# Differential attention with a feed-forward part on one core: the values product by Strassen's seven products

## The chip, the core and the metric

The kernel runs on one core of one Trainium2 chip. The metric is the device time of one execution in microseconds. Every engine of the core (TensorE for matmuls, VectorE, ScalarE, GpSimd) works through its own list of instructions in order, and SyncE issues most DMAs in the order of its own queue. In the profile they are PE, DVE, ACT, POOL and SP.

## The reference

The input x has 2048 tokens of 256 numbers, in float32. What is computed, cut to what matters:

```python
def attn(h):                       # h = layernorm(x)
    qkv = h @ Wqkv_w.T + Wqkv_b
    # 16 query heads as 8 pairs, 8 key heads as 4 pairs, D = 128; values 4 x 256
    p1 = softmax(causal(q[..., 0] @ k[..., 0].T / sqrt(D)))
    p2 = softmax(causal(q[..., 1] @ k[..., 1].T / sqrt(D)))
    o = (p1 - lam * p2) @ v        # 8 query pairs; two of them share keys and values
    o = o * rsqrt(mean(o * o) + eps) * subln_w * (1 - lambda_init)
    return o.reshape(S, 2048) @ out_w.T + out_b
x = x + layernorm(attn(layernorm(x)))
x = x + layernorm(ffn(layernorm(x)))   # Hadamard transforms, silu(gate) * up, down; 256 -> 1024 -> 256
```

## The kernel before

The work goes in four groups (`g`), one for each pair of key heads with its values. For a group, queries, keys and values of all 2048 tokens are projected from the normalised input (`project_heads`, `project_values`); two query pairs share the group's keys, and the program interleaves the rows of both, so that a tile of 128 tokens gives two half tiles of 64 tokens by two pairs.

The attention runs unit by unit. A `Unit` is one tile of 128 tokens for the first eight tiles (both halves, `ns` = 2), and one half tile for the other eight, so a group has 24 units and the whole kernel 96. The first group goes from short rows to long, the others from long to short. In the step of a unit, these things stand in each engine's list:

- `scores` (L267): matmuls of the unit's queries with all keys up to the diagonal, for two softmaxes, into PSUM tiles `sc` of 1024 columns, of which there are three. VectorE empties each into `e` and keeps the running minimum (L282, L293); ScalarE takes the exponential (L308).
- `combine` (L340): VectorE forms e0 + cf * e1 for the unit before.
- `turn` and `arrive` (L360, L365, L375): the probabilities are turned around for the values product, in blocks of 32x32 on VectorE and by a write to DRAM (`dr`) and four reads back (`pt`).
- `values` (L391), for the unit three steps back (`LAG`): for every tile of 128 keys a matmul with the turned probabilities as weights and the values as the moving operand, 128 rows by 256 columns, added up in a PSUM tile `po`.
- ScalarE copies the result and sums its squares (L404, L407), GpSimd forms the factor and scales (`inverse`, L418 to L421), `turn_out` and `arrive_out` turn the result around by VectorE and DRAM (L434, L439, L449), `project_out` multiplies it with the output weights (L458), and `accumulate` adds it to `acc` (L468).

The order is written out by hand: the tables `before`, `mid`, `between` and `after` say at which step a projection, a part of the folding of the feed-forward weights (`transform`, L618, on GpSimd, in steps 7 to 35), or a piece of the feed-forward part stands. The feed-forward part runs on blocks of 256 tokens, from the last block to the first, and begins while the last units are worked on.

Of the kernel before, what the change touches and what calls it, by code (L numbers as in the profile page):

```python
# [16 lines left out]
P = 128  # L17
# [15 lines left out]
LAG = 3  # L33
# [15 lines left out]
def kernel(  # L49
# [58 lines left out]

    x2 = x.rearrange("(b t s q) d -> b s q t d", t=2, s=2, q=64)
    outv = out.rearrange("(b t s q) d -> b s q t d", t=2, s=2, q=64)  # L110


    with ExitStack() as actx:
# [6 lines left out]
        ps_s = actx.enter_context(tc.tile_pool(name="ps_s", bufs=3, space=PSUM))  # L120
        ps_o = actx.enter_context(tc.tile_pool(name="ps_o", bufs=2, space=PSUM))
# [3 lines left out]
        qT = [qkp.tile([P, NT, 2, 2, 64], F32, name=f"q{m}") for m in range(2)]  # L125
        kT = [qkp.tile([P, S], F32, name=f"k{m}") for m in range(2)]
        vt = qkp.tile([P, NT, HID], F32, name="v")

# [4 lines left out]
        loaded = {}  # L133

        def load_qkv(g, engines, count=4):

            if g not in loaded:
                wq = xtp.tile([P, 2, 1024], F32, tag="wq", name=f"wq_{g}")
                loaded[g] = wq, xtp.tile([P, 256], F32, tag="vb", name=f"vb_{g}"), list(range(4))
            wq, _, left = loaded[g]  # L140
            for _ in range(count):
                k = left.pop(0)
                engines[k % len(engines)].dma_start(wq[:, :, ts(k, 256)], wqkv[4 * g + k])

        def load_vbias(g):
            nc.gpsimd.dma_start(loaded[g][1], vbias[:, ts(g, 256)].to_broadcast([P, 256]))
# [10 lines left out]

        def scale_wo(g):
            for c in range(2):
                nc.vector.tensor_scalar(  # L160
                    wos[g][:, :, c, :],
                    wos[g][:, :, c, :],
                    colv[:, C_SUBLN + c : C_SUBLN + c + 1],
                    1.0 - LAMBDA_INIT,
                    ALU.mult,
                    ALU.mult,
                )

        def project_heads(g, nb, j2, both=True, n=512):

            wq = loaded[g][0]
            cols4 = ts(nb, n)
            xb, lo = divmod(nb * n, 512)
            nt = n // P
            pp = ps_s.tile([P, 1024], F32, tag="sc", name=f"pp_{g}_{nb}_{j2}_{n}")
            for h in range(2):
                j = 2 * j2 + h
                for c in range(2):
                    nc.tensor.matmul(  # L179
                        pp[:, 512 * h : 512 * h + n],  # L180
                        lhsT=wq[:, c, ts(j, P)],
                        rhs=xnT[:, xb, c, lo : lo + n],
                        start=(c == 0),
                        stop=(c == 1),
                    )
            for h in range(2):
# [4 lines left out]
                if j < 4:  # L191
                    dst = qT[h][:, ts(nb, nt), :, j2, :].rearrange("d t s q -> d (t s) q")
                    src = src.rearrange("d (t q) -> d t q", q=64)
                else:
                    dst = kT[h][:, cols4]
# [6 lines left out]
        def project_values(g, nb):  # L202

            wq, vb, _ = loaded[g]
            pp = ps_s.tile([P, 1024], F32, tag="sc", name=f"pv_{g}_{nb}")
            for t in range(4):
                for c in range(2):
                    nc.tensor.matmul(  # L208
                        pp[:, ts(t, 256)],
                        lhsT=xnT[:, nb, c, ts(t, P)],  # L210
                        rhs=wq[:, c, 768:1024],
# [6 lines left out]
                vb.unsqueeze(1).to_broadcast([P, 4, 256]),  # L218
                ALU.add,
            )  # L220


        class Unit:
            def __init__(self, g, i, subs):
                self.g, self.i, self.subs = g, i, subs
                self.ns = len(subs)
                self.nk = i + 1
                self.L = [i * P + 64 * (s + 1) for s in subs]
                self.at = [a * self.nk * P for a in range(self.ns)]

                self.ng = self.nk if self.ns == 2 else (self.nk + 1) // 2
                self.n = f"{g}_{i}_{subs[0]}"
# [19 lines left out]
        def scores(u, half):  # L252

            for a, m in u.half(half):
# [5 lines left out]
                for c, w in enumerate(cuts(L)):  # L260
# [4 lines left out]
                    for k, lo in enumerate(los):  # L265
                        ww = w - lo if k == len(los) - 1 else step
                        nc.tensor.matmul(  # L267
                            sc[:, 512 * k : 512 * k + ww],
                            lhsT=qT[m][:, u.i, u.subs[a]].rearrange("d p q -> d (p q)"),
# [35 lines left out]
        def exponentials(u, half):  # L305
# [10 lines left out]
            if half:  # L316

                u.ed = sm.tile([P, 2], F32, tag="ed", name=f"ed_{u.n}", bufs=8)
                nc.scalar.activation(
                    u.ed[:, : u.ns], u.d[:, : u.ns, 0], AF.Square, scale=16.0 * math.sqrt(EPS)  # L320
                )

        def pad(u):

            lo, hi = u.L[0], (u.at[1] if u.ns == 2 else 256 * u.ng)
            if hi > lo:
                nc.gpsimd.memset(u.es[0][:, lo:hi], 0.0)
# [16 lines left out]
        def move(u, moved):  # L344

            if u:
                turn(u)
            if moved:
                arrive_out(moved)
            if u:  # L350
                arrive(u)

        def turn(u):
# [3 lines left out]
            e, x = u.es  # L357
            ng = u.ng
            order = "p (r g c) -> p r g c" if u.ns == 2 else "p (g r c) -> p r g c"
            nc.vector.transpose(  # L360
                x[:, : 256 * ng].rearrange("p (g c r) -> p r g c", g=ng, r=2),
                e[:, : 256 * ng].rearrange(order, g=ng, r=2),
            )
            dr = dram.tile([NT // 2, 4, 32, 4, 64], F32, tag="dr", name=f"dr_{u.n}")
            nc.sync.dma_start(  # L365
                dr[:ng].rearrange("g b q a w -> (b q) g (a w)"),
                x[:, : 256 * ng].rearrange("p (g w) -> p g w", g=ng),
            )
            u.dr = dr

        def arrive(u):
            ng, dr = u.ng, u.dr
            u.pt = ep.tile([P, S], F32, tag="pt", name=f"pt_{u.n}")
            for a in range(4):
                nc.sync.dma_start(  # L375
                    u.pt[ts(a, 32), : 256 * ng].rearrange("p (k w) -> p k w", w=64),
                    dr[:ng, :, :, a, :].rearrange("g b q w -> q (g b) w"),
                )

        def values(u, part=None):  # L380

            whole = [(a, kc) for a in range(u.ns) for kc in range(u.nk)]
            cut = len(whole) // 2
            if part != 1:
                u.po = None
            todo = whole if part is None else (whole[:cut], whole[cut:])[part]
            u.po = u.po or ps_o.tile([P, 512], F32, tag="o", name=f"po_{u.n}")
            ptv = u.pt[:, : 256 * u.ng].rearrange("p (g q r) -> p g r q", q=P, r=2)
            for a, kc in todo:
                g, r = (kc, a) if u.ns == 2 else (kc // 2, kc % 2)  # L390
                nc.tensor.matmul(  # L391
                    u.po[:, ts(a, HID)],
                    lhsT=ptv[:, g, r, :],
                    rhs=vt[:, kc, :],
                    start=(kc == 0),
                    stop=(kc == u.i),
                )
            if part == 0:
                return

            if (u.g, u.i) not in outs:
                outs[u.g, u.i] = op.tile([P, 2, HID], F32, tag="osb", name=f"osb_{u.g}_{u.i}")
            u.osb = outs[u.g, u.i][:, u.subs[0] : u.subs[0] + u.ns, :]
            nc.scalar.copy(u.osb.rearrange("p s e -> p (s e)"), u.po[:, : u.ns * HID])  # L404
            u.ss = sm.tile([P, 2], F32, tag="ss", name=f"ss_{u.n}")
            for a in range(u.ns):
                nc.scalar.activation(  # L407
                    u.po[:, ts(a, HID)],
                    u.po[:, ts(a, HID)],
                    AF.Square,  # L410
                    accum_out=u.ss[:, a : a + 1],
                )

        def inverse(u):

            f = sm.tile([P, 2], F32, tag="f", name=f"f_{u.n}")
            w = sm.tile([P, 2], F32, tag="u", name=f"u_{u.n}")
            nc.gpsimd.tensor_tensor(w[:, : u.ns], u.ss[:, : u.ns], u.ed[:, : u.ns], ALU.add)  # L418
            nc.gpsimd.tensor_tensor(f[:, : u.ns], w[:, : u.ns], mhalf[:, : u.ns], ALU.pow)  # L419
            for a in range(u.ns):  # L420
                nc.gpsimd.tensor_scalar(  # L421
                    u.osb[:, a, :], u.osb[:, a, :], f[:, a : a + 1], 16.0, ALU.mult, ALU.mult
                )

        outs = {}

        def complete(u):
            return u and u.subs[-1] == 1

        def turn_out(u):  # L430

            osb = outs[u.g, u.i]
            xo = op.tile([P, 512], F32, tag="xo", name=f"xo_{u.n}", bufs=1)
            nc.vector.transpose(  # L434
                xo.rearrange("p (g c r) -> p r g c", g=2, r=2),
                osb.rearrange("p r (g c) -> p r g c", g=2),
            )
            dr = dram.tile([2, 4, 32, 4, 64], F32, tag="do", name=f"do_{u.n}")
            nc.sync.dma_start(  # L439
                dr.rearrange("g b q a w -> (b q) g (a w)"),  # L440
                xo.rearrange("p (g w) -> p g w", g=2),
            )
            u.do = dr

        def arrive_out(u):
            dr = u.do
            u.oT = op.tile([P, 2, 2, P], F32, tag="oT", name=f"oT_{u.n}")
            for a in range(4):
# [592 lines left out]
```

## Time and profile before

| | |
|---|---|
| median of three runs | 1440.66 us (1440.43 to 1441.46) |
| span of the profiled execution | 1438.7 us |
| its own time beside the span | not listed on the page |
| busy: PE, DVE, ACT, POOL | 1429.8, 1028.8, 507.9, 360.9 us |
| largest groups on PE | values L391 488.1 us, scores L267 478.2, projections L179 170.6, output projection L458 121.0 |
| DMA | 210.79 MB, mean 147 GB/s |

A line of a group names the source line, the engine, the operation, what it writes and reads, the shapes and the count, then busy time and the mean duration in nanoseconds, then the idle time before it and what ended it. A line of the waits names who waited for whom, the total, the number of times and the longest. The profiled execution is one more run of the same program; its span goes from the first to the last instruction.

### The profile page before, as it was taken

The page shows a single profiled execution, that of the slowest core. Times are in us where ns is not written, and L with a number is a line of the kernel's source. Part 1 is how long each engine was busy: PE and PEld are TensorE (multiplying, and loading weights), DVE is VectorE, ACT ScalarE, POOL GpSimd, SP SyncE. Part 2 cuts the span into 40 slices and gives each one's busy share as a digit, 9 for nine tenths or more (in the row PEclk, how much of TensorE's full clock was granted, in tenths as well). Part 3 has the DMA queues.
Part 4 walks back from the last instruction along what each step waited for, and adds up shares of the span by engine and source line. Part 5 has one row for each costly group of instructions (what it writes and reads, how often), then busy time and mean ns, then how long its engine had stood idle before and what let it go on. Part 6 is the DMA issues. An engine that isn't in the chain of part 4 may idle for free.

```text
span 1438.7 us, 17597 instructions
## 1 busy us (share of the span) xinstructions
PE 1429.8 (99%) x5436; PEld 1037.6 (72%) x5436; DVE 1028.8 (72%) x2285; ACT 507.9 (35%) x1114; POOL 360.9 (25%) x683
## 2 busy tenths in 40 slices
PE   9999999999999999999999999999999999999998
PEld 7567767756766777776677776675777777888887
DVE  6588798847656888644967779545877799766774
ACT  3453433323133334333433334323424445531111
POOL 2037724830028921011111111111111121121110
PEclk9999999999999999999999999999999999999999
DMA  5379889856667797832788887631999999732120
GB/s 147 73 169 202 195 179 219 178 93 139 149 135 146 162 214 173 169 86 63 155 183 180 170 201 165 132 81 52 210 202 193 193 191 190 170 94 81 52 59 15
DMA packets 501436, 210.79 MB, mean 147 GB/s; under 512 B 396032, under 2 KB 499456, under 8 KB 501216
## 3 DMA queue, kind: packets, MB, share of 16 engines
q1 hardware_dynamic: 498128, 200.73, 65.9%
q0 software_dynamic: 2352, 8.26, 2.1%
q8 instruction: 44, 0.72, 0.2%
q10 hardware_dynamic: 864, 0.68, 0.2%
q14 instruction: 48, 0.39, 0.1%
HBM read 111.05 MB, written 98.57 MB: 146 GB/s over the span
## 4 chain that ended last, share of the span: by engine, by line
PE 98%; DVE 1%; DMA 0%; POOL 0%; issue 0%; ACT 0%; POOLq 0%; DVEq 0%
PE po L391 32%; PE sc L267 31%; PE pp L179 11%; PE pout L458 8%; PE gu L721 8%; PE pd L756 4%; PE pv L208 4%; DMA vb<-in_vbias 0%; PE warm L494 0%; DVE e L282 0%; DVE e L340 0%; DVE e L360 0%; DVE v L215 0%; PE pst L523 0%; ACT q L198 0%
## 5 line engine op out<-in xcount | busy, mean ns | idle before, releaser
L391 PE MATMUL po<-v,pt 128*128 128x256 f32 x2176 | 488.1, 379 | 0.0
L267 PE MATMUL sc<-k,q 128*128 128x512 f32 (+7 forms) x1280 | 478.2, 519 | 1.5 <-DVE last L293 0.6
L391 PEld LDWEIGHTS po<-v,pt 128*128 128x128 f32 x2176 | 425.7, 196 | 59.6 <-issue 11.1
L267 PEld LDWEIGHTS sc<-k,q 128*128 128x128 f32 x1280 | 237.8, 190 | 214.3 <-issue 182.4
L308 ACT ACTIVATE e<-e,last 128x192 f32<-128x192 f32 (+28 forms) x256 | 299.5, 1171 | 221.6 <-DVE last L293 202.6
L282 DVE TENSOR_SCALAR_CACHE_REDUCE e<-sc 128x1024 f32<-128x1024 f32 (+15 forms) x248 | 231.2, 932 | 176.6 <-PE sc L267 175.7
L418 POOL TENSOR_TENSOR u<-ss,ed 128x1 f32<-128x1 f32 (+1 forms) x96 | 20.0, 208 | 747.1 <-ACT po L407 747.0
L404 ACT COPY osb<-po 128x256 f32<-128x256 f32 (+1 forms) x96 | 42.6, 444 | 465.2 <-PE po L391 464.2
L340 DVE SCALAR_TENSOR_TENSOR e<-e,cf,e 128x64 f32<-128x64 f32 (+31 forms) x128 | 173.9, 1380 | 3.4
L360 DVE STREAM_TRANSPOSE e<-e 128x1536 f32<-128x1536 f32 (+7 forms) x96 | 166.7, 1737 | 7.4 <-DVE e L340 0.5
L179 PE MATMUL pp<-xnT,wq 128*128 128x512 f32 (+1 forms) x408 | 170.6, 568 | 0.3 <-DVE xnT L510 0.3
L179 PEld LDWEIGHTS pp<-xnT,wq 128*128 128x128 f32 x408 | 77.0, 190 | 78.3 <-issue 74.8
L458 PE MATMUL pout<-wo,oT 128*128 128x256 f32 x512 | 121.0, 379 | 0.1
L282 DVE TENSOR_SCALAR_CACHE_REDUCE e<-sc,mx 128x320 f32<-128x320 f32 (+13 forms) x128 | 97.1, 759 | 21.0 <-PE sc L267 8.0
L458 PEld LDWEIGHTS pout<-wo,oT 128*128 128x128 f32 x512 | 97.2, 190 | 13.2 <-issue 0.4
L293 DVE CUSTOM_DVE_ANT_0 e<-sc,mask,mx 128x64 f32<-128x64 f32 x248 | 70.5, 284 | 8.8
L734 ACT ACTIVATE hT<-gu,colv 128x256 f32<-128x256 f32 x64 | 26.9, 471 | 120.5 <-PE gu L721 120.5
L721 PE MATMUL gu<-fxnT,wgate 128*128 128x256 f32 x256 | 65.7, 379 | 0.0
L721 PE MATMUL gu<-fxnT,wup 128*128 128x256 f32 x256 | 65.7, 379 | 0.0
L421 POOL TENSOR_SCALAR osb<-osb,f 128x256 f32<-128x256 f32 x128 | 62.7, 490 | 11.8
L419 POOL TENSOR_TENSOR f<-u,mhalf 128x1 f32<-128x1 f32 (+1 forms) x96 | 58.3, 608 | 7.5
L740 DVE SCALAR_TENSOR_TENSOR hT<-gu,colv,hT 128x256 f32<-128x256 f32 x64 | 30.6, 478 | 40.5 <-ACT hT L734 40.5
(101 smaller groups left out, 1097.5 us busy)
## 6 DMA issues: line engine op xcount, KB each, us to landing
dr<-e SPq DMA_DIRECT2D x20, 1024.0 KB, 4.7
pt<-dr SPq DMA_DIRECT2D x80, 256.0 KB, 5.8
dr<-e SPq DMA_DIRECT2D x20, 896.0 KB, 4.4
pt<-dr SPq DMA_DIRECT2D x80, 224.0 KB, 5.0
do<-xo SPq DMA_DIRECT2D x64, 256.0 KB, 4.1
oT<-do SPq DMA_DIRECT2D x256, 64.0 KB, 2.6
dr<-e SPq DMA_DIRECT2D x20, 768.0 KB, 4.4
pt<-dr SPq DMA_DIRECT2D x80, 192.0 KB, 4.3
```

Of the source, the lines that this page charges most:

```text
L179: nc.tensor.matmul(pp[:, 512 * h : 512 * h + n], lhsT=wq[:, c, ts(j, P)], rhs=xnT[:, xb, c, lo : lo + n], start=(c == 0), stop=(c == 1),)
L267: nc.tensor.matmul(sc[:, 512 * k : 512 * k + ww], lhsT=qT[m][:, u.i, u.subs[a]].rearrange("d p q -> d (p q)"), rhs=kT[m][:, at + lo : at + ...
L282: nc.vector.tensor_scalar(dst, src, 1.0, best, ALU.mult, ALU.min, accum_out=u.mx[:, k0, c : c + 1],)
L293: nc.vector.tensor_tensor_reduce(e[:, L - 64 : L], sc[:, tail : tail + 64], mask, 1.0, best, ALU.add, ALU.min, accum_out=u.last[:, k0 : k0 ...
L308: nc.scalar.activation(e, e, AF.Exp, bias=u.last[:, 2 * a + m : 2 * a + m + 1], scale=-1.0, accum_out=u.d[:, a, m : m + 1],)
L340: nc.vector.scalar_tensor_tensor(e0, e1, cf[:, a : a + 1], e0, ALU.mult, ALU.add)
L360: nc.vector.transpose(x[:, : 256 * ng].rearrange("p (g c r) -> p r g c", g=ng, r=2), e[:, : 256 * ng].rearrange(order, g=ng, r=2),)
L391: nc.tensor.matmul(u.po[:, ts(a, HID)], lhsT=ptv[:, g, r, :], rhs=vt[:, kc, :], start=(kc == 0), stop=(kc == u.i),)
L419: nc.gpsimd.tensor_tensor(f[:, : u.ns], w[:, : u.ns], mhalf[:, : u.ns], ALU.pow)
L421: nc.gpsimd.tensor_scalar(u.osb[:, a, :], u.osb[:, a, :], f[:, a : a + 1], 16.0, ALU.mult, ALU.mult)
L458: nc.tensor.matmul(u.pout[:, :HID], lhsT=u.oT[:, c, p, :], rhs=wos[u.g][:, p, c, :], start=(p == 0 and c == 0), stop=(p == 1 and c == 1),)
L721: nc.tensor.matmul(ps[:, ts(2 * j + n, 256)], lhsT=ffn[which][:, c, ts(fc, P)], rhs=xnT[:, c, :], start=(c == 0), stop=(c == 1),)
```

## The change

The unit of the values product becomes a block of 256 tokens (two tiles, with their two query pairs as rows `r`) against a block of 256 keys. A block on the diagonal takes six matmuls of 256 columns. A block off the diagonal (there are 28 in a group) is taken as a product of two 2x2 matrices of 128-wide blocks, by seven products in the form of Strassen and Winograd. Values are now the weights and the probabilities the moving operand, so the result arises transposed.

- The sums of the values, `vm`, are formed by GpSimd after each `project_values`; the sums of the probabilities, `sums`, by GpSimd for each block, four additions of 256 columns, up to two blocks ahead (`NSUM`).
- Turned probabilities are fetched block by block (`fetch`), up to five blocks ahead (`NA`), after all units of a block of rows have been turned.
- The products gather in four PSUM banks, `z0` to `z3`. For them, `sc` has two tiles instead of three. `collect` puts the result together on ScalarE, VectorE and GpSimd once for each block of rows (32 in all).
- The output need not be turned any more. The sum of its squares runs along partitions now, and is formed by squares on ScalarE, a transpose and a reduction on VectorE, and a way through DRAM in small transfers (`squares`, `scales`); the factor is applied after the output projection.
- Queries are kept in a ring of two blocks of 512 tokens, and are projected shortly before they are used.
- These later steps are put into the program by a clock that counts the matmuls' time (`later`, `poll`). Projections, folding steps and the begin of the feed-forward part move by some steps, and its back product uses the `z` banks.

The core of the diff:

```diff
-LAG = 3
+NA = 5
+NSUM = 2
+RIPE = 3
-        ps_s = actx.enter_context(tc.tile_pool(name="ps_s", bufs=3, space=PSUM))
-        ps_o = actx.enter_context(tc.tile_pool(name="ps_o", bufs=2, space=PSUM))
+        ps_s = actx.enter_context(tc.tile_pool(name="ps_s", bufs=2, space=PSUM))
+        ps_z = actx.enter_context(tc.tile_pool(name="ps_z", bufs=1, space=PSUM))
...
+            nc.gpsimd.tensor_tensor(t1, b12, b11, ALU.subtract)
+            nc.gpsimd.tensor_tensor(t2, b22, t1, ALU.subtract)
+            nc.gpsimd.tensor_tensor(t4, b21, t2, ALU.subtract)
+            nc.gpsimd.tensor_tensor(t3, b22, b12, ALU.subtract)
...
+        def sums(n):
...
+            nc.gpsimd.tensor_tensor(s1, a21, a22, ALU.add)
+            nc.gpsimd.tensor_tensor(s2, s1, a11, ALU.subtract)
+            nc.gpsimd.tensor_tensor(s4, a12, s2, ALU.subtract)
+            nc.gpsimd.tensor_tensor(s3, a11, a21, ALU.subtract)
...
+        def values(n):
+            b, j = items[n]
+            p = b.p[j]
+            if j < b.i:
+                s, v, m = b.s[j], vv[:, j], vm[:, j]
+                last = j == b.i - 1
+                product(b, 0, 0, v[:, 0, 0, :], p[:, 0, 0], last)
+                product(b, 2, 0, v[:, 1, 0, :], p[:, 0, 1], False)
+                product(b, 2, 256, m[:, 3, :], p[:, 1, 1], False)
+                product(b, 1, 0, m[:, 0, :], s[:, 0, :], last)
+                product(b, 0, 256, m[:, 1, :], s[:, 1, :], last)
+                product(b, 3, 0, vv[:, j, 1, 1, :], s[:, 3, :], False)
+                product(b, 1, 256, m[:, 2, :], s[:, 2, :], last)
+                return
...
+        def collect(b):
...
+                nc.scalar.copy(w[:, 0, :], b.z[0][:, :256])
+                nc.scalar.copy(w[:, 1, :], b.z[1][:, :256])
+                nc.vector.tensor_tensor(w[:, 2, :], b.z[0][:, 256:], w[:, 0, :], ALU.add)
+                nc.vector.tensor_tensor(w[:, 3, :], b.z[1][:, 256:], w[:, 2, :], ALU.add)
+                nc.gpsimd.tensor_tensor(
+                    b.o[:, 1],
+                    w[:, 2:4, :],
+                    w[:, 1:2, :].to_broadcast([P, 2, 256]),
+                    ALU.add,
+                )
+                nc.vector.tensor_tensor(
+                    b.o[:, 0], b.z[2].rearrange("p (r q) -> p r q", r=2), w[:, 0::3, :], ALU.add
+                )
+                nc.vector.tensor_tensor(o1, b.z[3], o1, ALU.add)
...
+            b.sq = op.tile([P, 1024], F32, tag="sq", name=f"sq_{b.n}", bufs=1)
+            nc.scalar.activation(b.sq, b.o.rearrange("p h r q -> p (h r q)"), AF.Square)
+            nc.gpsimd.tensor_tensor(b.sq[:, :512], b.sq[:, :512], b.sq[:, 512:], ALU.add)
+            later(3.0, squares, b)
...
         for which, begin_at, steps in (
-            ("up", 5, range(7, 15)),
-            ("gate", 17, (18, 19, 20, 21, 22, 22, 23, 23)),
+            ("up", 7, range(8, 16)),
+            ("gate", 18, (19, 20, 20, 21, 22, 22, 23, 23)),
             ("down", 26, (28, 29, 29, 30, 30, 31, 32, 33, 34, 35)),
         ):
```

## The prediction

> **What bounds the kernel now.** I read the page's engine totals and its chain first. In the busy line, each engine has its busy time, its share of the span and its instructions; the second line is the chain that ended last, by engine.
>
> ```profile
> span 1438.7 us, 17597 instructions
> PE 1429.8 (99%) x5436; PEld 1037.6 (72%) x5436; DVE 1028.8 (72%) x2285; ACT 507.9 (35%) x1114; POOL 360.9 (25%) x683
> ...
> PE 98%; DVE 1%; DMA 0%; POOL 0%; issue 0%; ACT 0%; POOLq 0%; DVEq 0%
> ```
>
> TensorE is the bound from end to end. A busy TensorE need not be at its peak, so next comes the chain in order of time (start, length, what):
>
> ```profile
> 340.00 3.43 PE sc L267 x8
> 343.43 6.91 PE po L391 x32
> 350.34 1.73 PE pout L458 x8
> ...
> 1353.59 13.81 PE gu L721 x64
> ```
>
> A matmul call is recorded as two instructions: 2176 records of L391 for the 1088 calls that the loops make (4 groups of 272). So 6.91 us for 32 records is 0.432 us per call of 256 columns, and 3.43 for 8 is 0.858 per call of 512. Scores, values and the feed-forward part all run at 0.00169 us a column. Counted in the program, all calls of before have 847,104 columns: 1429 us at that rate, of a span of 1438.7. Nothing but start and tail is lost, so a removed matmul is worth its full time as long as the other engines keep up.
>
> Whether they do is read from stretches (us, then PE, PEld, DVE, ACT and POOL busy, clock, DMA share, GB/s):
>
> ```profile
> 690.00:760.00 70.00, 70.00 (x262) 49.96 (x261) 55.28 (x93) 24.56 (x45) 9.12 (x22) 1.00 0.91 184
> 430.00:510.00 80.00, 80.00 (x300) 57.53 (x300) 58.71 (x105) 27.77 (x55) 69.03 (x101) 1.00 0.75 157
> 104.00:124.00 20.00, 20.00 (x83) 15.57 (x82) 18.56 (x34) 7.84 (x20) 11.66 (x20) 1.00 0.95 189
> ```
>
> VectorE is at 79% under long rows (690 to 760) and 93% in the worst stretch, and TensorE doesn't wait even there. GpSimd is idle on the whole but at 86% while a weight matrix is folded (430 to 510).
>
> **What is removed.** A 256x256 block took 8 calls of 256 columns and takes 7; there are 28 off-diagonal blocks per group, 112 in all. A diagonal block keeps 6. The program's own count agrees: 2726 calls become 2614, all other columns stay. 112 x 0.432 = 48.4 us, so the floor is a span of 1390.3.
>
> The page has no time of its own for the profiled execution, only its span; the median of the three runs, 1440.66, lies 2.0 us above it, and I add these 2.0 at the end: 1392.3.
>
> A product now streams the probabilities in runs of 32 elements and its diagonal form writes two runs of 128; no row shows either. Between no cost and, should only the 64 diagonal calls double, 28 us, I take none, from L391, whose weights were read with a stride of two at the common rate.
>
> **What is added, by engine.** These rows give the prices (busy, mean ns):
>
> ```profile
> L434 DVE STREAM_TRANSPOSE xo<-osb 128x512 f32<-128x512 f32 x64 | 45.3, 707 | 2.7 <-DMA df<-xf 2.7
> L468 DVE TENSOR_TENSOR acc<-pout,acc 128x256 f32<-128x256 f32 x48 | 20.1, 420 | 2.9 <-PE pout L458 2.9
> L215 DVE TENSOR_TENSOR v<-pv,vb 128x1024 f32<-128x1024 f32 x16 | 19.5, 1220 | 23.6 <-PE pv L208 22.7 <-DMA vb<-in_vbias 0.9
> L100 DVE SCALAR_TENSOR_TENSOR y<-y,rsc,acc 128x256 f32<-128x256 f32 x16 | 7.1, 482 | 1.0 <-POOL rsc L93 0.7
> ```
>
> VectorE loses 64 output transposes (45.3) and 64 accumulations (26.9). It gains 56 adds of 256 (0.42), 56 of 512 (0.69, between the L468 and L215 rows), 32 transposes of 512 (0.707), 32 reductions of 512 (about 0.6, taken near the same rows) and 32 small ones (0.2), 64 scalings of 256 (0.48), four more query copies and 16 wider transposes (together 7): 23.5 + 38.6 + 22.6 + 25.6 + 30.7 + 7 = 148. The net is +76, so about 1105 us in 1390: 79% instead of 72%.
>
> GpSimd loses L418 to L421 (141 us) and gains 448 sums. The additions of the weight fold have their shape (min/median/max ns):
>
> ```profile
> L618 POOL TENSOR_TENSOR t_gate<-t_gate x56: 612/727/2712, 244.3 to 299.3; 128x256 f32<-128x256 f32 x56
> ```
>
> 448 x 0.727 = 326; 64 sums over the values, 47 at most; three adds of 512 per row block (92 at 1.45), 134; smaller ones 38. GpSimd goes from 361 to about 765 us, still half of the span, but its work stands in the way of the products now. The 2712 is an addition that met a combine of VectorE: it took about 2 us longer. A combine pays as well, as the same form shows in an undisturbed and in a folding stretch:
>
> ```profile
> L340 DVE SCALAR_TENSOR_TENSOR e<-e,cf,e 128x1984 f32<-128x1984 f32 x1 | 2.3, 2286 | 0.0
> L340 DVE SCALAR_TENSOR_TENSOR e<-e,cf,e 128x1984 f32<-128x1984 f32 x1 | 2.7, 2720 | 0.0
> ```
>
> That is 0.43 us per combine that meets GpSimd, 55 us of VectorE time if all 128 do, in stretches with slack mostly free.
>
> ACT trades copies and squares of about the same size and stays near 35%. DMA drops the output turn (64 x 256 KB out, and 256 x 64 KB back) and gains 320 small transfers; probabilities move the same bytes. SP's queue gets ten small transfers per row block, each behind whatever is queued; with five probability blocks in flight I cost this at nothing. If that cover is gone, the next block's fetch is late by the 4 to 6 us that such transfers take to land.
>
> **What of it reaches the path.** I counted matmuls, VectorE and GpSimd work in the changed program's order and priced them as above.
>
> Start: the first six units have 52 us of matmuls (69 before, as projections move later) against 49 on VectorE. Between 0 and 10 us of waiting; I take 4, since 93% was harmless in the 104 to 124 stretch, but with three score tiles instead of two.
>
> Group change: five units of the third group (the second to the sixth) stand where the old values are used up and the new ones not ripe. Before they had 70.0 us of matmuls, which is the 690 to 760 stretch with 55.3 on VectorE. After, 41 fewer value calls and 4 more output calls leave 54.0; VectorE has 55.3 - 4.9 (4 transposes, 5 accumulations) + 9.5 = 59.9. So VectorE is the bound there by 6 us, from 0 (its lag is carried by the two score tiles, 1.7 us of matmuls each) to 8 (five combines stretched by 0.43). I take 3, and the same in the fourth group: 6.
>
> Weight fold: units 9 to 15 hold 60 fold additions, 28 sums and 15 us of other GpSimd work, 79 us beside 72 of matmuls. Units 30 and 31 hold 40 fold additions, 20 sums and 7 us, 51 beside 30; two blocks of sums made ahead cover some 13 of these 21. GpSimd also waits in its queue, and the sums stand behind that now:
>
> ```profile
> POOL t_gate L618 <- DMA dw_up<-x_up: 14.4, 1, 14.4
> POOL raw_down L587 <- DVE x_gate L637: 10.5, 1, 10.5
> ```
>
> Between 0 and 40; I take 4 + 6 = 10.
>
> Collecting a row block: VectorE's last add waits for an add of 1.45 on GpSimd and does 0.69 meanwhile, so it stands still 0.8 us, or up to 3.7 if four sums are ahead. Behind it in VectorE's order are a transpose and the emptying of score tiles, for which TensorE waits. 28 such blocks: 0 to 104 us. TensorE has half a unit's scores in between, so I take 0.3 each: 8.
>
> Sum: 1390.3 + 4 + 6 + 10 + 8 = 1418.3, and 1420.3 with the 2.0.
>
> [...] The stretches of before have a granted clock of 1.00, and TensorE's longest wait in the trace is 1.5 us, at the start; by these rows waiting costs only itself. [...]
>
> **Rivals.** Full gain: the waits hide behind the queue of score tiles as they do now. For it, VectorE at 93% is harmless in before; against it, the two stretches where another engine has more work than TensorE. It gives 1392 to 1400.
>
> Slower: the collect's hand-off from VectorE to GpSimd and back. With 20 us for start, group change and fold, 28 us of gain are left, so it decides from 1.0 us per block. At 1.8 us (GpSimd inside a group of sums every second time, with no third score tile to bridge it) it costs 50: 1390.3 + 20 + 50 + 2 = 1462. For it: both engines are strictly in order here, and GpSimd doubles its work. Against it: half a unit of scores, 2 to 3.5 us of matmuls, stands between a collect and the next product.
>
> No change: waits of 46 to 51 us, 1438 to 1443. The change not doing what it says is excluded by the count of calls.
>
> **Numbers.** Forecast (1400 to 1438) 0.46, full gain 0.17, no change 0.06, slower 0.31. What a measurement here can tell from no change is about 0.2%, 2.9 us. Faster is 0.63, same 0.06, slower 0.31. The range leaves out the best of the full gain and the upper half of the slower case: 1396 to 1456; the forecast's own is 1400 to 1438.
>
> **What would show it.** TensorE has 5212 records, still 0.432 per product; VectorE is near 1105 busy and GpSimd near 765 or more. Idle time before products should name GpSimd's sums in units 9 to 15 and 30 to 31, and before scores VectorE at the group changes. The prediction is wrong if products take over 0.45 us each, if waits are under 10 us or over 48, or if most of them lie at the collects.

## The result and the profile after

The changed kernel takes 1679.55 us (median of four runs, 1674.75 to 1683.17) beside 1440.65 of the kernel before (1440.43 to 1441.46): a ratio of 1.165, with a 95% interval of 1.163 to 1.168. It is 239 us slower where 20 us of gain were forecast. The profiled execution took 1676.31 us, 1.8 more than its span.

The page of the changed kernel, the lines that answer to those of before: span, busy time by engine, the chain that ended last, and the granted clock in tenths over 40 slices.

```profile
span 1674.5 us, 18117 instructions
PE 1472.2 (88%) x5212; PEld 1002.7 (60%) x5212; DVE 1131.9 (68%) x2433; ACT 489.6 (29%) x914; POOL 775.3 (46%) x1071
...
PEclk8999889899999999999899999999999999799999
...
PE 55%; DVE 24%; POOL 6%; DMA 5%; issue 4%; SPq 3%; ACT 3%; DVEq 0%; POOLq 0%; ACTq 0%
```

The removed work is gone: 5212 records. Yet TensorE went from 98% of the chain to 55%, VectorE from 1% to 24%, and VectorE is *less* loaded than before as a share (68% against 72%). TensorE's busy time even rose, 1429.8 to 1472.2, with 48 us of matmuls fewer, and the clock row has eights and a seven: part of the matmuls ran slower.

I worked out the loss from the matmul records: the time from one record's start to the next, less what its columns take at the common rate. It comes to 288 us, as good as the whole of the 284 us by which the span lies above the floor of 1390.3; the same count gives under 6 us for the kernel before. Some 223 of the 288 are idle TensorE and some 65 matmuls at half rate (where a gap ends and slow matmuls begin is a matter of the count; other ways of drawing the line give 52 to 75 for the second part). Of the idle time, some 136 us lie between two score matmuls and 31 before an output projection. The loss lies all along the kernel, not at the group changes and the fold alone.

The waits (who <- on whom: us in total, times, longest us) say what TensorE and VectorE stand for:

```profile
PE sc L147 <- DVE e L330: 66.4, 21, 8.7
...
PE po L147 <- DVE e L330: 28.8, 9, 8.0
...
DVE o L532 <- POOL o L523: 26.5, 27, 4.9
...
PE gu L147 <- DMA fxnT<-df: 16.4, 1, 16.4
...
PE z L147 <- POOL sum L446: 4.7, 4, 1.8
```

TensorE waits for VectorE to empty score tiles (L330). It hardly waits for the sums of GpSimd (4.7 us). What VectorE does meanwhile stands in the timeline of one step (start, length, what; in brackets the idle time before):

```profile
784.25 2.29 DVE L395 SCALAR_TENSOR_TENSOR e<-e,cf,e 128x1984 f32<-128x1984 f32 x1
786.46 0.41 DVE L521 TENSOR_TENSOR w<-z,w 128x256 f32<-128x256 f32 x1
786.98 0.42 DVE L522 TENSOR_TENSOR w<-z,w 128x256 f32<-128x256 f32 x1
787.50 0.69 DVE L529 TENSOR_TENSOR o<-z,w 128x512 f32<-128x512 f32 x1
788.78 0.69 DVE L532 TENSOR_TENSOR o<-z,o 128x512 f32<-128x512 f32 x1 [0.58 <-POOL o L523]
789.39 2.30 DVE L406 STREAM_TRANSPOSE e<-e 128x2048 f32<-128x2048 f32 x1
791.61 1.18 DVE L330 TENSOR_SCALAR_CACHE_REDUCE e<-sc 128x1024 f32<-128x1024 f32 x1
```

TensorE over the same time:

```profile
783.27 3.60 PE L147 MATMUL sc<-k,q 128*128 128x512 f32 x8
792.87 4.84 PE L147 MATMUL sc<-k,q 128*128 128x512 f32 x8 [6.00 <-DVE e L330]
```

At 783.27 TensorE fills both score tiles in 3.6 us. VectorE takes 7.4 us for combine, collect and transpose before it empties the first, at 791.61. TensorE stands still for 6 us, and the next eight records take 4.84 us instead of 3.4: the clock fell as well (the granted clock is 0.50 from 789.02 to 795.84). The stretch around it (us, then PE, PEld, DVE, ACT and POOL busy, clock, DMA share, GB/s) has VectorE at 75% and a mean granted clock of 0.83:

```profile
780.00:830.00 50.00, 37.25 (x103) 21.71 (x103) 37.42 (x62) 17.24 (x26) 11.18 (x11) 0.83 0.22 64
```

Of the 28 collects, 22 have a wait of TensorE of 0.7 us or more beside them. A smaller form, combine and transpose alone (4.6 us against a cover of 3.4), comes with some of the units of long rows, such as the wait of 1.93 us at 805.35. A second place is the output projection:

```profile
818.36 6.07 PE L147 MATMUL po<-wo,o 128*128 128x256 f32 x16 [4.48 <-DVE e L330]
824.27 1.88 PE L147 MATMUL sc<-k,q 128*128 128x512 f32 x4
```

Its result takes one of the two score tiles; it waited 4.48 us for that, and ran at 6.07 us for eight calls, which at 0.432 each are 3.46.

### The profile page after: what moved, and what is told of

It reads as the page before. It is cut to its first block, busy times and chain, and to the rows that moved or that the text cites. A ratio compares the mean times of both kernels' runs of the same rounds, so it can differ in the third digit from the quotient of the medians.

```text
span 1674.5 us, 18117 instructions
## 1 busy us (share of the span) xinstructions
PE 1472.2 (88%) x5212; PEld 1002.7 (60%) x5212; DVE 1131.9 (68%) x2433; ACT 489.6 (29%) x914; POOL 775.3 (46%) x1071
## 4 chain that ended last, share of the span: by engine, by line
PE 55%; DVE 24%; POOL 6%; DMA 5%; issue 4%; SPq 3%; ACT 3%; DVEq 0%; POOLq 0%; ACTq 0%
PE sc L147 17%; PE z L147 13%; PE pp L147 7%; PE po L147 6%; PE gu L147 6%; DVE e L330 5%; DVE e L395 5%; DVE e L406 4%; PE pd L147 3%; PE pv L147 2%; POOL t_down L764 2%; DMA pt<-dr 1%; POOL o L523 1%; DVE y L596 1%; SPq L427 1%
## 5 line engine op out<-in xcount | busy, mean ns | idle before, releaser
L330 DVE TENSOR_SCALAR_CACHE_REDUCE e<-sc 128x1024 f32<-128x1024 f32 (+15 forms) x248 | 231.5, 934 | 105.0 <-PE sc L147 103.5
L147 PE MATMUL z<-sum,vm 128*128 128x256 f32 x672 | 186.1, 385 | 5.2 <-POOL sum L446 4.7
L147 PE MATMUL z<-pt,v 128*128 128x256 f32 x704 | 182.4, 382 | 1.5 <-DMA pt<-dr 1.5
L446 POOL TENSOR_TENSOR sum<-pt 128x256 f32<-128x256 f32 x112 | 96.8, 864 | 174.1 <-PE z L147 93.2
L406 DVE STREAM_TRANSPOSE e<-e 128x1536 f32<-128x1536 f32 (+5 forms) x96 | 170.5, 1776 | 6.2 <-DVE e L395 0.5
L147 PEld LDWEIGHTS z<-pt,v 128*128 128x128 f32 x704 | 133.4, 192 | 41.7 <-issue 16.9
L147 PE MATMUL po<-wo,o 128*128 128x256 f32 x512 | 126.9, 404 | 28.9 <-DVE e L330 28.8
L147 PEld LDWEIGHTS z<-sum,vm 128*128 128x128 f32 x672 | 127.9, 192 | 27.9 <-POOL sum L446 6.6
L147 PEld LDWEIGHTS po<-wo,o 128*128 128x128 f32 x512 | 103.3, 204 | 49.9 <-DVE e L330 32.9
L330 DVE TENSOR_SCALAR_CACHE_REDUCE e<-sc,mx 128x320 f32<-128x320 f32 (+13 forms) x128 | 97.1, 759 | 34.6 <-PE sc L147 22.8
L147 PE MATMUL z<-sum,v 128*128 128x256 f32 x352 | 106.1, 383 | 3.9 <-DVE o L532 2.6
L448 POOL TENSOR_TENSOR sum<-pt,sum 128x256 f32<-128x256 f32 x112 | 91.2, 815 | 8.8
L147 PE MATMUL gu<-fxnT,wgate 128*128 128x256 f32 x256 | 68.3, 391 | 19.1 <-DMA fxnT<-df 16.4
```

What stands on the lines that cost most here:

```text
L147: nc.tensor.matmul(o, lhsT=lhsT, rhs=rhs, start=start, stop=stop, **kw)
L330: nc.vector.tensor_scalar(dst, src, 1.0, best, ALU.mult, ALU.min, accum_out=u.mx[:, k0, c : c + 1],)
L406: nc.vector.transpose(y[:, : 256 * n].rearrange("p (g b k q) -> p k g b q", g=n, b=4, k=2), e[:, : 256 * n].rearrange("p (g k b q) -> p k ...
L446: nc.gpsimd.tensor_tensor(s1, a21, a22, ALU.add)
L448: nc.gpsimd.tensor_tensor(s4, a12, s2, ALU.subtract)
```

## The experiments

Every run stands beside the kernel before on the same chip, which took 1440.5 to 1441.1 each time. All are single runs; the changed kernel's own four lie 8.4 us apart, so a difference of that size says little. Theory A: TensorE runs in step with VectorE, since two score tiles don't bridge the work that VectorE does between two emptyings. The first four runs put it against B, the output projection's place in a score tile and its hand-off, and C, the added work of GpSimd.

**Two tiles in the kernel before.**

```diff
-ps_s = ... tc.tile_pool(name="ps_s", bufs=3, space=PSUM)
+ps_s = ... tc.tile_pool(name="ps_s", bufs=2, space=PSUM)
```

> The kernel before with two score tiles in PSUM instead of three, nothing else. Theory A (with two tiles TensorE cannot run past VectorE's combine and transpose, some 4.7 us in one piece): the clean line of before breaks, 30 to 150 us longer, with TensorE waiting for the row that empties the score tiles and the granted clock below 1. Theory B (the output projection's hand-off to ScalarE and VectorE in the changed kernel is what costs): under 10 us longer, since before empties the output projection a step later. Theory C (GpSimd's sums): no change.

1571.55 us, 130.5 more. The matmuls and every other instruction are those of the kernel before. Two of its waits, and what the same view has with three tiles, where the first isn't there:

```profile
PE sc L267 <- DVE q L200: 28.1, 14, 5.6
PE sc L267 <- DVE e L282: 20.0, 30, 1.1
```
```profile
PE sc L267 <- DVE e L282: 0.5, 1, 0.5
```

Projections write into tiles of the same pool (`pp` has the tag `sc`), so L200, which reads a projected query out of one, is an emptying too.

So the third score tile, which the change trades for accumulators, is worth more than twice what the seven products save.

**Three tiles in the changed kernel.** The accumulators share two banks in pairs (so they add up what doesn't belong together), and the back product of the feed-forward part has two banks instead of four.

```diff
-b.z[k] = ps_z.tile([P, 512], F32, tag=f"z{k}", ...)
+h = b.z.get((k + 2) % 4)
+b.z[k] = h if h is not None else ps_z.tile([P, 512], F32, tag=f"z{k % 2}", ...)
...
-ps_s ... bufs=2
+ps_s ... bufs=3
```

> The changed kernel with three score tiles: z2 and z3 share the banks of z0 and z1, so the values' results are mixed up while every matmul and every other instruction stays (the feed-forward back product has two banks instead of four). Theory A: most of the 284 us over the floor go, time 1420 to 1520. Theory B: VectorE still stands before the scaled output for some 120 us, and 1560 or more remains. Theory C: over 1600.

1588.23 us: 91 less, but 196 above the 1392.3 of the matmuls, and above the range that A gave (it lies in B's, which the next run decides). The third tile is a large part, not the whole.

**The scaled output off VectorE.**

```diff
-nc.vector.scalar_tensor_tensor(y[:, t, :], po[:, t, 1, :], b.f[...], y[:, t, :], ALU.mult, ALU.add)
+nc.scalar.activation(b.o[:, 0, t, :], po[:, t, 1, :], AF.Copy, scale=b.f[...])
+nc.gpsimd.tensor_tensor(y, y, b.o[:, 0], ALU.add)     # once, after both t
```

> The changed kernel with the scaled output formed by ScalarE and GpSimd alone: VectorE no longer stands behind the output projection's matmuls (29 waits, 121 us in the changed kernel). Theory B: 80 to 150 us less, 1530 to 1600. Theory A: the output projection still takes one of two score tiles, 10 to 50 us less. Theory C: no change within 15 us, or longer, as GpSimd has one more addition per block.

**The sums of the probabilities left out.** The products take unsummed operands.

```diff
-nc.gpsimd.tensor_tensor(s1, a21, a22, ALU.add)    # and s2, s3, s4
+return                                            # off the diagonal
```

> The changed kernel with the sums of the probabilities left out (the products take the turned probabilities themselves, so the result is not the reference's): GpSimd loses some 330 us of work. Theory C: more than 100 us less. Theories A and B: 10 to 40 us less, from the stretches where the weight fold and the sums meet on GpSimd and from combines that no longer meet it.

1657.13 and 1655.57 us, 22 and 24 less, in the ranges of theory A: B and C are small.

**The collect's stop.** This is the slower rival of the prediction.

```diff
-nc.gpsimd.tensor_tensor(b.o[:, 1], w[:, 2:4, :], ..., ALU.add)
+nc.vector.tensor_tensor(b.o[:, 1], w[:, 2:4, :], ..., ALU.add)
```

> The changed kernel with one edit: the collect's add of 512 elements that GpSimd makes between two adds of VectorE is made by VectorE itself, so that VectorE never stops for GpSimd there. VectorE works 28 x 0.69 = 19 us more. Theory A (TensorE runs in step with VectorE, because two score tiles bridge nothing; every stop of VectorE counts): the 26 us that VectorE waits there go, 19 us of its work come: 5 us more to 25 us less, 1655 to 1685. Theory H (the hand-off is dear: behind each stop the clock falls too): 50 to 100 us less, 1580 to 1630.

> The changed kernel with three score tiles (the four accumulators of the products share two banks), and the collect's add on VectorE as in the run before. Against three tiles alone (1588.2). Theory A: with a third tile short stops are bridged, so this moves little: 1575 to 1595. Theory H (what is left with three tiles are the stops of VectorE for GpSimd's sums at the collect, 4.6 us at the largest gap of TensorE): 1530 to 1565.

1681.14 us with two tiles (1.6 more, which is nothing beside the spread), 1578.07 with three (10 less). The stop was there, 26.5 us, close to the 1.0 us per block from which the rival was to decide; taking it away gives nearly nothing. That this is because the add then lengthens the same piece of VectorE's work is my reading; no run shows it by itself.

**Four edits at once.**

```diff
 # the edits of the collect and of the scaled output, and:
-turn(mixed)                      # ahead of scores(new, 1)
+turn(mixed)                      # behind it; and one more feed() there
...
-for c in range(4): nc.sync.dma_start(b.fin[...], ...)   # right behind dq, de
+later(5.0, gather, b, dr, de)                           # gather issues them
```

> The changed kernel with three score tiles and four edits that keep VectorE and SP's queue from standing in the way: the collect's add on VectorE, the scaled output by ScalarE and GpSimd instead of VectorE, the transpose of the probabilities behind the emptying of the second half's scores instead of before it, and the small transfers of a row block issued in two goes, the second 5 us later. If what is left with three tiles is VectorE's work between two emptyings of score tiles (theory A), it falls under the kernel before: 1400 to 1440. If VectorE is short of time as such in long stretches, wherever its work stands: 1500 to 1560. If the clock or something else holds TensorE: no less than 1570.

1582.16 us, no better than one of them. A miss for A in the form that I had given it. The waits show why:

```profile
POOL sq L538 <- ACT sq L537: 223.1, 27, 20.6
...
PE sc L147 <- DVE e L330: 38.3, 19, 4.5
...
ACT sq L537 <- DMA df<-xf: 32.3, 2, 20.3
...
PE z L147 <- POOL sum L446: 30.4, 7, 14.0
```

The wait for emptied score tiles fell from 64.1 us (three tiles alone) to 38.3. But the products' wait for their sums rose from 10.8 to 30.4. GpSimd is hardly busier (781.8 us against 778.4); it stands more, 223 us before the squares' add where it was 95. The wait of 14.0 us, in the timeline at 1351, is such a case: the sum stood in GpSimd's order behind that add, the add waited for ScalarE's square, and the square 20.3 us for a transfer of the feed-forward part, whose source `xf` takes the same buffer (tag `sq`). Which of the four edits brought the rest isn't shown.

**Is TensorE still the bound?**

```diff
 product(b, 1, 256, m[:, 2, :], s[:, 2, :], last)
+product(b, 1, 256, m[:, 2, :], s[:, 2, :], last)   # the first one with stop=False
```

> The changed kernel with one of the seven products of each off-diagonal block made twice: 112 calls more, 48.4 us of TensorE at the rate of the profile; nothing else is changed (the values are no longer the reference's). If TensorE is the bound: 48 us more, 1728. Theory A (TensorE waits for VectorE most of the time that it loses, and these calls fall into such waits): 0 to 25 us more, 1680 to 1705. If the calls keep the clock up and fill the gaps, even less than 1680.

1708.82 us, 29.3 more for 48.4 us of matmuls, a little over what theory A gave. Some six tenths of what a product costs reach the end, even here; the loss is elsewhere and much larger.

**Leaving out the added work, with three tiles and with two.**

```diff
 # free GpSimd: no sums, and in transform():
+return
 # no finish: in collect()
-(the adds, squares, transpose, reduction, ten transfers, scales)
+nc.scalar.copy(o0, b.z[2]); nc.scalar.copy(o1, b.z[3]); b.f = mhalf
```

> Three score tiles (accumulators share two banks), the collect's add on VectorE, and GpSimd freed of its two large pieces of work: the sums of the probabilities (448 adds) and the weight fold (168 adds) are left out; the same products are made on unsummed operands. Against the same without this (1578.1). If what is left with three tiles is GpSimd standing in the way of products and of VectorE (theory G): 1440 to 1490. Theory A (VectorE's work between the emptyings): 1530 to 1570, as leaving out the sums gave 24 us with two tiles.

> Three score tiles, and a row block's finish left out: the collect is two copies of ScalarE out of the accumulators, no squares, no transpose, no reduction and no small transfers follow, and the output projection takes a constant for its scale factors, 14 us after the collect as before. GpSimd's sums and the weight fold stay. Against three tiles alone (1588.2). Theory A (VectorE's 28 collects and 32 squares, some 130 us of work between emptyings): 1470 to 1520. Theory G: no less than 1550.

> Three score tiles, with both left out: GpSimd's sums and weight fold, and the finish of a row block. What is added to the kernel before is then the wider transposes, the probabilities' new form, and the output projection in a score tile. If VectorE and GpSimd explain what three tiles leave: 1395 to 1430, that is the 1392.3 of the matmuls and a little. If a cause that nobody named holds TensorE (the clock by itself, the products' operands, the output projection's place): 1460 or more.

> The changed kernel with its two score tiles, and the same two parts left out (sums and weight fold; finish). The kernel before lost 130.5 us by two tiles. If the costs add up: as much above the run before it, 1525 to 1560. If two tiles cost much only together with the added work of VectorE and GpSimd: 1430 to 1480.

| | us | against |
|---|---|---|
| three tiles, collect on VectorE | 1578.07 | |
| the same, GpSimd freed | 1546.95 | -31 |
| three tiles | 1588.23 | |
| the same, no finish | 1485.18 | -103 |
| the same, GpSimd freed too | 1457.70 | -27 more |
| two tiles, no finish, GpSimd freed | 1568.46 | -111 (changed kernel); +111 (the line above) |

The loss has come apart: the finish of 32 row blocks 103 us, GpSimd 27 to 31, the third tile 91 to 111. With three tiles and both parts left out, 1457.70 lies between the two ranges expected: 65 us above 1392.3 remain, which I didn't take apart by runs. In the trace they are 62.5 us of idle TensorE and 7.1 at half rate; the longest gap is one of 12.6 us at the start of the feed-forward part. Their cause stays open.

**What of the finish?** Three tiles, one part left out each:

```diff
 # run 13, the collect: its adds become copies of ScalarE
 # run 14, what follows it: no squares, transfers, scale factors (b.f = mhalf)
 # run 15: only the ten transfers
-nc.sync.dma_start(...)   # dq, de, fin
+ss is reduced from part, without them
```

> Three score tiles, and only the collect's four adds of VectorE and one of GpSimd left out (two copies of ScalarE in their place); squares, small transfers and scale factors stay. Against 1588.2 with them and 1485.2 with the whole finish left out. If the collect's pieces and its stop for GpSimd are most of the 103 us: 1500 to 1530. If the rest of the finish is: 1550 to 1580. Run 6 took the stop away for 10 us, so I expect 1545 to 1570.

> Three score tiles, the collect as it is, and what follows it left out: squares, their transpose and reduction, the ten small transfers, the scale factors (a constant takes their place, 14 us after the collect). If these are most of the 103 us: 1500 to 1530, and the next run tells which of them. If the collect is: 1560 to 1580.

> Three score tiles, and of a row block's finish only the ten small transfers left out; the scale factors come from the partial sums as they lie (not the right ones). If SP's queue, held up by them, delays the probabilities' fetches and through them the products: 1510 to 1540. If VectorE's work is what costs: 1575 to 1590.

1549.35, 1534.59 and 1563.70 us, the second a little over its range and the third between its two: the collect is worth 39 us, what follows 54, of it 24.5 for the transfers. Together they make 93 of the 103. No single part decides. The parts hold work of VectorE, adds of GpSimd, copies and squares of ScalarE and SP's transfers at once; the transfers apart, these runs don't say which engine's share costs.

**The same pieces in the kernel before**, once in one piece, once spread:

```diff
 # at the end of values(), once per row block; d is a part of acc
+nc.vector.tensor_tensor(d[:, 256:512], ...)     # 0.42
+nc.vector.tensor_tensor(d[:, :256], ...)        # 0.42
+nc.gpsimd.tensor_tensor(d[:, 512:], ...)
+nc.vector.tensor_tensor(d[:, :512], ...)        # 0.69
+nc.vector.tensor_tensor(d[:, :512], d[:, :512], d[:, 512:], ...)
+nc.vector.transpose(d[:, 512:], d[:, :512])
+nc.vector.tensor_reduce(dc, d[:, 512:], ...)
 # spread: the same in a list, and behind each emptying in scores()
+one_piece()
```

> The kernel before, three score tiles, with the changed kernel's collect and squares added once per row block behind its last product: two adds of 256, two of 512 with GpSimd's add of 512 ahead of the last, a transpose and a reduction of 512, all on the accumulator of the output (whose values are spoilt by it). 32 x 3.7 us of VectorE work and 32 stops for GpSimd; no transfers. Theory A (such work between emptyings is what costs): 1460 to 1520. If three tiles bridge it and the cost in the changed kernel comes from its transfers or from elsewhere: 1440 to 1450.

> The kernel before with the same collects and squares as the run before it (three score tiles, the accumulator of the output spoilt in the same way), but one instruction at a time: each of the six pieces stands behind the emptying of another score tile, so that the next tile is emptied after at most 1.4 us of other work; the pieces of the very last row block are left out. Against 1540.0 in one piece and 1441.1 without. If the piece between two emptyings is what costs (theory A): 1441 to 1460. If it is the amount of VectorE's work or its stops for GpSimd: 1510 to 1540.

In one piece: 1540.02 us, 98.9 more and above the range expected, with nothing taken from the kernel before, its three tiles included. VectorE, then TensorE, at one such place:

```profile
759.60 0.42 DVE L420 TENSOR_TENSOR acc<-acc 128x256 f32<-128x256 f32 x1
761.41 0.69 DVE L422 TENSOR_TENSOR acc<-acc 128x512 f32<-128x512 f32 x1 [1.39 <-POOL acc L421]
762.14 0.69 DVE L423 TENSOR_TENSOR acc<-acc 128x512 f32<-128x512 f32 x1
762.87 0.71 DVE L424 STREAM_TRANSPOSE acc<-acc 128x512 f32<-128x512 f32 x1
763.61 0.69 DVE L425 TENSOR_REDUCE dc<-acc 128x16 f32<-128x512 f32 x1
764.22 1.22 DVE L217 TENSOR_TENSOR v<-pv,vb 128x1024 f32<-128x1024 f32 x1
```
```profile
758.23 3.38 PE L269 MATMUL sc<-k,q 128*128 128x512 f32 x8
765.49 5.18 PE L269 MATMUL sc<-k,q 128*128 128x512 f32 x8 [3.87 <-DVE v L217]
```

Spread: 1462.69 us, 22.2 more, a little over the range of A and far from the other. VectorE is as busy in both (1135.9 and 1137.5 us), so the amount isn't what costs; the long piece is. The stop for GpSimd, 1.4 us each time, is part of that piece, and it too shrinks when something else stands in between; these two runs don't part it from the work around it. In one piece, then spread:

```profile
DVE acc L422 <- POOL acc L421: 44.4, 32, 1.4
...
PE sc L269 <- DVE e L284: 39.3, 14, 4.7
```
```profile
PE sc L275 <- DVE e L290: 7.5, 5, 5.2
...
DVE acc L434 <- POOL acc L432: 5.4, 3, 2.7
```

**Spread in the changed kernel**, two tiles, with the scaled output off VectorE:

```diff
-nc.vector.tensor_tensor(w[:, 2, :], ...)
+pend.append(lambda: nc.vector.tensor_tensor(w[:, 2, :], ...))   # and so on; flushed ahead of values(n)
```

> The changed kernel with its two score tiles; the collect's adds, the squares' transpose and their reduction each stand behind the emptying of another score tile, as far as the next products allow, and the scaled output is made by ScalarE and GpSimd. Against 1657.1 with the latter alone. Combine and transpose of the probabilities (4.6 us) still stand in one piece. If spreading helps with two tiles as well: 1590 to 1630. If two tiles are lost on the combine and transpose anyway: 1645 to 1670.

1712.99 us, 56 more than without it (1657.13): a miss. The adds of the collect empty the accumulators, and the next row block's products wait for these:

```profile
PE z L147 <- DVE o L547: 44.5, 16, 5.2
...
PE z L147 <- DVE w L545: 11.9, 4, 8.5
...
PE z L147 <- DVE o L550: 9.4, 4, 7.7
```

In the kernel before TensorE waited for none of the spread pieces; here the accumulators have no second set, so the collect must be soon *and* short. No version here beats the kernel before; the best of the changed one that leaves nothing out is the scaled output off VectorE, 1657.13.

## Why the prediction was wrong

**The floor held.** 5212 records; in the timeline the 12 records of a diagonal block's products, from 780.68 to 783.27, take 2.59 us, 0.432 per call. Strided operands cost nothing there, as assumed.

**Prices held, mostly.** VectorE was forecast at 1105 and is at 1131.9, GpSimd 765 and 775.3. The collect's 512-wide add on GpSimd takes 1.27, its sums 0.72 alone.

**The step that failed is the cover.** The prediction took a load below 100% in a stretch as the test of whether TensorE waits, and added only what exceeded it. For the third score tile there was no term: it appears as a remark, "but with three score tiles instead of two", and "its lag is carried by the two score tiles". The first run priced it at 130.5 us in the kernel before, whose worst stretch had VectorE at 93% and no waiting. What decides is the longest piece between two emptyings against the filled tiles: 7.4 us against 3.6 in the timeline above. The profile of before would have given it: combine and transpose take 4.6 us for long rows, and two tiles hold 3.4 us of scores.

```profile
L360 DVE STREAM_TRANSPOSE e<-e 128x2048 f32<-128x2048 f32 x20 | 46.4, 2318 | 2.0 <-DVE e L340 0.5
...
L340 DVE SCALAR_TENSOR_TENSOR e<-e,cf,e 128x2048 f32<-128x2048 f32 x4 | 9.4, 2351 | 0.1
```

**The collect's term of 8 us was mis-sized.** With three tiles the collect measured 39 us, and what follows it another 54 (103 for the whole finish). The prediction counted only VectorE's stop for GpSimd, 0.3 us a block; the stop was near 1.0 us a block, but removing it gave nothing to 10 us. The rest of the 39 comes with its work, which the prediction had put at no cost as work hidden under TensorE. So the slower rival came out on the right side with the wrong mechanism; it would have given 1462.

**The output projection had no term.** Its result moved from a tile of its own to a score tile. 22 us came back when VectorE's part of its emptying was taken away; the wait for the tile (29.2 us in that run) and the rest of the hand-off stayed.

**GpSimd's 10 us** measured 24 for the sums with two tiles, and 27 to 31 for sums and fold with three. It did not show as products waiting for sums in the folding units, as forecast (4.7 us in all), but, where I looked, in VectorE's pieces. Units 9 to 15, where the forecast set 4 us, lose some 33 (seven average units lose 21), and units 30 and 31 some 6, as forecast. A collect with three tiles, from the timelines of GpSimd and VectorE:

```profile
282.84 4.63 POOL L765 TENSOR_TENSOR t_gate<-t_gate 128x256 f32<-128x256 f32 x4
...
290.38 1.26 POOL L524 TENSOR_TENSOR o<-w 128x512 f32<-128x512 f32 x1
```
```profile
291.68 0.69 DVE L533 TENSOR_TENSOR o<-z,o 128x512 f32<-128x512 f32 x1 [4.58 <-POOL o L524]
```

Four fold additions and four sums stood ahead of the add, and VectorE stopped 4.58 us for it.

**Small transfers at nothing** were 24.5 us with three tiles. Those of a row block take 2.0 to 2.4 us to land in the changed kernel (medians of the four kinds, 0.5 to 8 KB), not 4 to 6; in the kernel before it is the fetches of probabilities, 192 to 256 KB each, that take 4.3 to 5.8. A part of the 24.5 is the first feed-forward product, which waits 8.4 us for its input without them and 14.7 with (16.4 in the changed kernel). That part is uncertain: with the finish and GpSimd's work left out it still waits 12.4.

**Start and group change.** The first six units lose 22 us (forecast 4; 5 of them are lost in the kernel before too), and the five units named at each of the two late group changes 27 to 29 (3 each). Five units of the average lose 15, so the group change is worse than the rest, but most of the loss lies elsewhere.

**The clock** had no term in the sum; matmuls at half rate are some 65 us of the loss. That waiting costs only itself was the wrong reading; it came from a kernel in which TensorE's longest wait was 1.5 us. The changed kernel has 30 stretches at half the clock.

## What to carry to other kernels

Before you trade a PSUM buffer for accumulators, compare the longest uninterrupted piece of work between two emptyings with the time that the producer needs to fill the buffers; the load of the emptying engine (72% before, 68% after) doesn't tell. New work for that engine is priced by where it stands: the same 3.4 us or so per row block cost 99 us in one piece and 22 spread between emptyings. And a gain of the bound engine, here 3%, is worth less once it must wait (some six tenths, by the run with eight products), while waits of a few microseconds were mostly followed by slower matmuls (in the changed kernel a stretch at half the clock begins within 5.5 us of the start of 28 of the 35 gaps of over 2 us).

## What the runs showed of the hardware

In the kernel before with collects in one piece, TensorE has 17 gaps of 2.78 to 4.91 us (from start to start, less what the columns take), each one before a score matmul or product; 15 of them are followed by a stretch in which the granted clock is one half, and the two without are 3.02 and 3.18 us long. No gap up to 1.76 us is. The stretch begins 2.3 to 5.0 us after the gap began, so it falls mostly on the matmuls after it, and lasts 3.4 us or a multiple. The timeline above has one such gap: TensorE stands for 3.87 us, and the eight records behind it take 5.18 us where the eight ahead of it took 3.38. The mean granted clock of that run is 0.979. But the length of the gap alone doesn't decide: in the kernel before with two tiles, gaps of 2.58 and 2.61 us were followed by such a stretch, and four of 2.83 to 3.30 weren't. In the changed kernel there are 30 stretches, 167 us long in all: 17 of 3.41 us, eight of 6.83, three of 10.24, one of 20.48 and, at the program's end, one of 3.48. The 29 ahead of that begin 2.5 to 5.5 us after a gap of 1.73 us or more began. Gaps of 1.73 and 1.95 us were followed by a stretch there, and six of 2.06 to 3.13 weren't. I had not expected that a loss of some 223 us in waits would bring another 65 or so with it.
